# Context of one slot block in four as three float16 products of split exponentials and values

## The chip, the cores and the metric

The kernel runs on one core of a Trainium2 chip. The metric is the device time of one execution in microseconds, and for a comparison the median over several executions. One core has a matrix engine (TensorE, PE in the profile; its weight loads are listed apart as PEld), a vector engine (VectorE, DVE), an activation engine (ScalarE, ACT), a general engine (GpSimd, POOL) and a sequencer that issues transfers (SyncE, SP). Each takes its own instructions in the order that the program fixed when it was built.

## The reference

Masked self-attention on 16 batches of 1024 tokens and 512 features, with 8 heads of 64, a residual sum, and queries, keys and values all made by the same matrix.

```python
xt = jnp.transpose(x, (0, 2, 1))                  # x: (16, 512, 1024)
q = xt @ Wq.T
qh = q.reshape(B, T, NH, dk).transpose(0, 2, 1, 3)
scores = scale * jnp.einsum('bhqd,bhkd->bhqk', qh, qh)
logits = (scores * cmask + (1.0 - cmask) * NEG) * rmask
attn = jax.nn.softmax(logits, axis=-1)
ctx = jnp.einsum('bhqk,bhkd->bhqd', attn, qh)
out = ctx.transpose(0, 2, 1, 3).reshape(B, T, D) @ Wo.T
return x + jnp.transpose(out, (0, 2, 1))
```

The mask holds 0 or 1, about half of each. A token whose mask is 0 gets the mean of all values; a token whose mask is 1 attends to the tokens whose mask is 1.

## The kernel before

**Slots.** For each batch the tokens with mask 1 are gathered into at most `C` = 544 slots: four blocks of 128 (`i` = 0 to 3) and a tail of 32, 16 or 0 (`A` slots in all: 544 in the first five batches, 528 up to the fourteenth, 512 in the last two). Matrix work is done on slots alone. All other tokens get one row per batch, made from the mean.

**Batch by batch.** `run` goes through the batches in a loop. While batch b's scores and context are made, the same passage makes the queries and values of batch b + 1, normalizes and projects batch b - 1, and gathers rows for b + 2. These pieces stand in a list `m`, each with a cost, and `fill` hands them out between the steps of batch b by shares that are written out by hand. The steps `S` are (p, i): pair p of heads (0 to 3), block i (0 to 3), and two more for the tail's scores. The Tile framework then fixes the order of each engine's instructions from the program order, from priorities (`high_priority`, `behind`) and from its own estimate of when each is ready.

**Queries.** `query` (L513) makes q from float16 halves of weights and rows, three products per pair; `qsplit` (L529 to L531) splits q into a high and a low float16 half, stored as high, low, high, and four transfers spread them over the tile `xx`, whose upper 64 partitions hold the halves in the other order.

**Values.** `value` transposes q's high and low halves into PSUM (`pv`, one of the two `pm` buffers), copies it to a float32 tile `v` on ScalarE (L572) and sums squares (L556, L557). The greatest sum of squares gives the shift of the softmax, `nm` (L639), and the checks on it (`MMAX`, L644).

**Scores and exponentials.** `scores` does four float16 products (L701) into one of two PSUM buffers `pss`, and one exponential on ScalarE (L705) that reads `pss` and writes a float32 tile `p` (128 x A, 12 buffers), with the sum of each row. The tail's scores (L676) use weights of 32 columns, four matmuls side by side.

**Context.** `attend` multiplies the values of a block by its exponentials, in float32: per block four matmuls with weights of 128 x 64 (two halves of the columns `g` by two heads `k`), the two heads writing to different halves of the partitions of `pav`. The matmuls of pair p are held back and run together at step (p + 1, 1), blocks 3, 2, 1, 0 in a row; then the tail's (L730) and a copy of the result to `c` on ScalarE (L734).

**After it.** `recip_sums`, `recip_rows` and `norm` make and apply the softmax's denominators, split the context into float16 halves `ch` and `cl` (L802, L803), `project` (L817) multiplies them by the output matrix and adds the rows (L822), and indirect transfers on GpSimd's queue scatter the result (L901).

**Queues.** SP's queue takes the direct transfers in program order; `later` puts a piece of work off to the start of the next step, which so far is used for the transfers of `qsplit` and of the tail. POOL's queue takes the gathers and scatters, one per step.

Of the kernel before, what the change touches and what calls it, by code (L numbers as in the profile page):

```python
# [10 lines left out]
F32 = mybir.dt.float32  # L11
# [8 lines left out]
P = 128  # L20
D = 512
# [15 lines left out]
MMAX = 60.0  # L37
# [6 lines left out]
HPO = 300  # L44


class Fast:
# [45 lines left out]
    def setup(self, mask_t):  # L93
# [30 lines left out]
        self.oht = fixed("oht", [P, B, TB, NB], F16)  # L124
# [11 lines left out]
        self.qt = fixed("qt", [P, 2, HG, CT])  # L136
        self.number = iota("number", [P, B - 2], [[1, B - 2]], 2, 0)
# [70 lines left out]
    def permute(self):  # L208

        nc, B = self.nc, self.B - 2  # L210
        at, mh = self.at16, self.later16
        each = self.sb([P, B, TB, B], F16, "ch", 2)
        nc.vector.tensor_tensor(each, at.unsqueeze(2).broadcast_to([P, B, TB, B]),
                                mh.rearrange("p b j -> p j b").unsqueeze(1).broadcast_to([P, B, TB, B]), ALU.mult)
        with nc.allow_low_precision(reason="one of the terms is 0 or 1, the others are 0"):
            nc.vector.tensor_reduce(self.later16, each, AX.X, ALU.add)
# [15 lines left out]
    def slots(self, b0, b1):  # L232
# [13 lines left out]
        for j in range(TB):  # L246
# [22 lines left out]
                                self.ionb.unsqueeze(1).broadcast_to([P, NC, NB]), ALU.is_equal)  # L269
        for b in range(B):  # L270
            nc.vector.tensor_tensor(self.oht[:, b0 + b], oh[:, b * TB:(b + 1) * TB, :],
                                    self.tok.unsqueeze(2).broadcast_to([P, TB, NB]), ALU.mult)
# [46 lines left out]
    def index(self, b):  # L319
        nc = self.nc  # L320
        s = self.st[b]
        ol = s["ol"]
        pi = self.pm([P, NB])
        for j in range(TB):
            self.pe = nc.tensor.matmul(pi, lhsT=ol[:, j, :], rhs=self.oht[:, b, j, :], start=(j == 0), stop=(j == TB - 1)).ins
# [78 lines left out]
    def gather_now(self, b, j):  # L404
        s = self.st[b]
        if j < 4:
            s["xa"].append(self.rows(s["idx"][:, j:j + 1], self.sb([P, D], F32, "xa", 13)))
        else:
            s["xt"] = self.rows(s["idx"][:s["A"] - 512, 4:5], self.sb([P, D], F32, "xt"))
# [64 lines left out]
    def xt(self, b, k):  # L474
# [4 lines left out]
        if n:  # L479
            x = s["xa"][k] if k < 4 else s["xt"]  # L480
            if b == 0:
                pt = self.ps_s.tile([P, 2, D], F32, tag="s", name="pss")[:, 0, :DC * n].rearrange("p (c n) -> p c n", c=DC)
            else:
                pt = self.pm([P, DC, n])
            for c in range(DC):
                self.pe = nc.tensor.transpose(pt[:, c, :], x[:n, c * P:(c + 1) * P], self.ident[:n, :n]).ins
# [34 lines left out]
    def qsplit(self, b, e):  # L521
# [5 lines left out]
        full = self.sb([P, 3, C], F16, "hl", 2)  # L527
# [3 lines left out]
        nc.vector.tensor_copy(hl[:, 2, :], hl[:, 0, :])  # L531
# [6 lines left out]
        def spread():  # L538
            lo, up = slice(0, DK), slice(DK, P)
            nc.sync.dma_start(out=xx[lo, 0:2, :], in_=hl[lo, 0:2, :])  # L540
            nc.sync.dma_start(out=xx[up, 0:2, :], in_=hl[lo, 1:3, :])
            nc.sync.dma_start(out=xx[lo, 2:4, :], in_=hl[up, 0:2, :])
            self.last_xx = nc.sync.dma_start(out=xx[up, 2:4, :], in_=hl[up, 1:3, :]).ins
# [15 lines left out]
    def value(self, b, e):  # L559
# [72 lines left out]
    def bottom(self, b, g):  # L632
# [6 lines left out]
        nc.vector.tensor_scalar(nm[:, :HG], pb, -SCALE, None, ALU.mult)  # L639
# [4 lines left out]
        nc.vector.tensor_scalar(okm, nm[:, :HG], -MMAX, None, ALU.is_ge)  # L644
        nc.vector.scalar_tensor_tensor(okm, nm[:, :HG], -MMIN, okm, ALU.is_le, ALU.mult)
# [15 lines left out]
    def scores(self, b, p, i):  # L661
# [8 lines left out]
        if i is None:  # L670
# [8 lines left out]
            t = self.sb([P, C], F32, "p", 12)[:, :A]  # L679
# [24 lines left out]
        t = self.sb([P, C], F32, "p", 12)[:, :A]  # L704
# [3 lines left out]
        return t  # L708

    def attend(self, b, p, i, ps):  # L710
# [6 lines left out]
        for g in range(2):  # L717
            for k in (1, 0) if i < 4 else range(2 if A == C else 1):
                cols = slice(g * CH, (g + 1) * CH)
                if i < 4:  # L720
                    with ExitStack() as st:
                        if self.group_first:

                            st.enter_context(self.behind(self.group_first))
                            st.enter_context(self.tc.high_priority(offset=HPO))
                        mm = nc.tensor.matmul(s["pav"][k * DK:(k + 1) * DK, g, :CH], lhsT=s["v"][p][:, i, k * DK:(k + 1) * DK],  # L726
                                              rhs=ps[k][:, cols], start=(i == 3), stop=(i == 0 and A == 512))
                    self.group_first = self.group_first or mm.ins
                elif A > 512:
                    nc.tensor.matmul(s["pav"][:, g, :CH], lhsT=s["vt"][p // 2][:, k, p % 2 * 2:p % 2 * 2 + 2, :],  # L730
                                     rhs=s["pt"][:, p % 2, cols], start=False, stop=(k == 1 or A < C))
        if i == 4:
# [44 lines left out]
    def norm(self, b, p):  # L777
# [4 lines left out]
        if p == 0:  # L782

            s["ch"] = self.sb([P, NP, 512], F16, "ch", 2) if b < self.B - 1 else self.xh[:, :, :512]
            s["cl"] = self.sb([P, NP, 512], F16, "cl", 2) if b < self.B - 1 else self.xl[:, :, :512]
# [15 lines left out]
        ch, cl = s["ch"][:, p, :], s["cl"][:, p, :]  # L801
# [7 lines left out]
    def product(self, ch, cl, cols, po=None, es=range(DC)):  # L809
# [5 lines left out]
        for e in es:  # L815
            for k, (a, w) in enumerate(((ch, wh), (ch, wl), (cl, wh))):
                nc.tensor.matmul(po[:cols.stop - cols.start], lhsT=a[:, e, cols], rhs=w[:, e, :],  # L817
# [14 lines left out]
    def late(self, b, j, tag="xi", bufs=8):  # L832

        self.post(lambda: self.late_now(b, j, *(("xg", 1) if j == 4 else (tag, bufs))), urgent=j == 4)

    def late_now(self, b, j, tag, bufs):
        s = self.st[b]
        idx = s["tails"][:len(self.group[b]) * CT] if j == 4 else s["idx"][:P if j < 8 else T - self.kept[b] - 3 * P, j:j + 1]
        s.setdefault("xi", {})[j] = self.rows(idx, self.sb([P, D], F32, tag, bufs)), idx

    def project_tail(self, b, *part):
# [6 lines left out]
        po = self.product(*s["ct"], slice(0, m), *part)  # L848
# [8 lines left out]
    def project_means(self, b):  # L857
# [9 lines left out]
        po = self.product(m[:, 0], m[:, 1], slice(0, n))  # L867
# [435 lines left out]
```

## Time and profile before

| | |
|---|---|
| median of 3 runs | 1032.48 us (1032.27 to 1036.74) |
| the profiled execution's own time | 1036.56 us |
| its span, first to last instruction | 1034.9 us |
| mean granted clock of TensorE | 0.993 |
| PE busy, share of the span | 989.3 us, 96% |
| DVE busy | 724.1 us, 70% |
| ACT busy | 659.2 us, 64% |
| POOL busy | 301.5 us, 29% |

The page gives, for each engine, the time in which at least one of its instructions ran; then the span in 40 slices; then groups of instructions by line, with the busy time of the group, the mean of one, and the idle time of the engine just before them and what ended it. Matmuls overlap each other, so the mean duration of a matmul is longer than the distance from one start to the next; what a stretch of matmuls costs is read from the starts in the timeline. The answers by window give the busy time of each engine in a stretch; the answers on waits give who waited for whom.

### The profile page before, as it was taken

The numbers are of one execution on the slowest core, as the hardware profiler recorded it, in microseconds if no ns is written. First come the engines' busy times: TensorE is split into PE (matmuls) and PEld (weight loads), VectorE is DVE, ScalarE is ACT, GpSimd is POOL, SyncE is SP. The second block draws the span as 40 slices with busy tenths as digits, with TensorE's granted clock in tenths as the row PEclk, the third lists the DMA queues.
The fourth block names the chain that finished last, engine by engine and source line by source line (L and its number), as shares of the span: only waits on it lengthen the run. The fifth ranks groups of instructions, "written<-read, shape, count | busy, mean of one in ns | idle before, by whom it ended". The sixth has DMA issues, their size and how long they took to land. (4 is left out here: it accounts for less than half of the span.)

```text
span 1034.9 us, 23506 instructions
## 1 busy us (share of the span) xinstructions
PE 989.3 (96%) x8455; PEld 686.2 (66%) x8455; DVE 724.1 (70%) x2410; ACT 659.2 (64%) x1702; POOL 301.5 (29%) x307
## 2 busy tenths in 40 slices
PE   7798999999999999999999999999999999999996
PEld 6576667666676766767666676766767666676563
DVE  6897668676675667876676787767677776666653
ACT  5876667657667665667667567666667666565550
POOL 3101013222311232333232333323233232326562
PEclk9899999999999999999999999999999999999998
DMA  6846556557654485575658665576665657455652
GB/s 206 224 135 184 139 137 162 174 160 205 175 133 131 138 244 167 154 208 142 197 158 217 181 174 170 155 202 187 164 211 147 195 166 193 140 142 186 195 187 85
DMA packets 78795, 177.73 MB, mean 172 GB/s; under 512 B 14688, under 2 KB 20576, under 8 KB 78672
## 3 DMA queue, kind: packets, MB, share of 16 engines
q1 hardware_dynamic: 57584, 108.40, 39.0%
q0 software_dynamic: 21088, 67.75, 20.9%
q8 instruction: 69, 1.13, 0.5%
q14 instruction: 54, 0.44, 0.1%
HBM read 91.49 MB, written 33.91 MB: 121 GB/s over the span
## 5 line engine op out<-in xcount | busy, mean ns | idle before, releaser
L705 ACT ACTIVATE p<-pss,nm 128x528 f32<-128x528 f32 (+2 forms) x512 | 359.3, 706 | 186.5 <-PE pss L701 176.6
L701 PE MATMUL pss<-xx 128*128 128x264 f16 (+2 forms) x2048 | 302.7, 277 | 6.3 <-ACT p L705 5.2
L726 PE MATMUL pav<-p,v 128*64 128x264 f32 (+2 forms) x2048 | 243.3, 390 | 0.0
L701 PEld LDWEIGHTS <-xx 128*128 128x128 f16 x2048 | 194.9, 99 | 64.2 <-issue 26.2
L726 PEld LDWEIGHTS pav<-p,v 128*64 128x64 f32 x2048 | 141.5, 137 | 85.6 <-issue 13.5
L901 POOL DMA_INDIRECT y_out<-xa,idx x68 | 73.5, 1081 | 282.3 <-PE pss L701 100.1
L513 PE MATMUL pm<-xh,wqh 128*128 128x264 f16 (+5 forms) x512 | 142.4, 278 | 3.7 <-DVE xa L822 3.1
L513 PE MATMUL pm<-xh,wql 128*128 128x264 f16 (+5 forms) x512 | 141.9, 277 | 0.0
L513 PE MATMUL pm<-xl,wqh 128*128 128x264 f16 (+5 forms) x512 | 141.8, 277 | 0.0
L395 POOL DMA_INDIRECT xa<-x_in,idx x68 | 67.4, 992 | 208.2 <-PE pss L701 91.8
L513 PEld LDWEIGHTS <-wqh 128*128 128x128 f16 x1024 | 98.3, 99 | 23.7 <-issue 7.1
L705 ACT ACTIVATION_READ_ACCUMULATOR p<-pss,nm 128x1 f32 x512 | 104.1, 203 | 0.0
L901 POOL DMA_INDIRECT y_out<-xi,idx x60 | 73.6, 1226 | 96.7 <-PE pss L701 27.6
L817 PE MATMUL pm<-woh,ch 128*128 128x512 f16 x240 | 91.1, 380 | 0.0
L817 PE MATMUL pm<-wol,ch 128*128 128x512 f16 x240 | 91.0, 379 | 0.0
L817 PE MATMUL pm<-woh,cl 128*128 128x512 f16 x240 | 91.0, 379 | 0.0
L395 POOL DMA_INDIRECT xi<-x_in,idx x60 | 62.5, 1042 | 93.6 <-PE pss L701 31.2
L516 ACT ACTIVATE q<-pm 128x264 f32<-128x264 f32 (+5 forms) x128 | 50.1, 391 | 58.1 <-PE pm L513 57.4
L822 DVE SCALAR_TENSOR_TENSOR xa<-pm,xa 128x512 f32<-128x512 f32 x60 | 41.3, 688 | 54.3 <-PE pm L817 50.6
L817 PEld LDWEIGHTS <-ch 128*128 128x128 f16 x480 | 46.0, 98 | 44.8 <-issue 0.9
L888 DVE TENSOR_TENSOR xi<-xi,ub 128x512 f32<-128x512 f32 (+1 forms) x60 | 40.8, 687 | 42.6 <-PE pss L701 42.3
L799 DVE TENSOR_TENSOR c<-c,rb 128x528 f32<-128x528 f32 (+2 forms) x64 | 45.4, 709 | 30.0 <-PE pm L513 16.3
(223 smaller groups left out, 1506.4 us busy)
## 6 DMA issues: line engine op xcount, KB each, us to landing
xx<-hl SPq DMA_DIRECT2D x224, 136.0 KB
xm<-x_nat_in SPq DMA_DIRECT2D x56, 512.0 KB
rb<-rd SPq DMA_DIRECT2D x72, 132.0 KB
rb<-rd SPq DMA_DIRECT2D x40, 136.0 KB
pt<-c SPq DMA_DIRECT2D x36, 132.0 KB
pt<-p SPq DMA_DIRECT2D x36, 132.0 KB
ub<-ud SPq DMA_DIRECT2D x16, 256.0 KB
xx<-hl SPq DMA_DIRECT2D x32, 128.0 KB
```

What stands on the lines that cost most here:

```text
L395: dma = self.nc.gpsimd.indirect_dma_start(out=tile[:n], out_offset=None, in_=self.x, in_offset=bass.IndirectOffsetOnAxis(ap=idx, axis=0))
L513: self.beat = nc.tensor.matmul(pq, lhsT=w[:, c, e * P:(e + 1) * P], rhs=xx[:, c, cols], start=(k == 0), stop=(k == 3 * DC - 1)).ins
L516: nc.scalar.activation(s["q"][:, e, cols], pq, AF.Copy, scale=1.0 / (SX * SW))
L701: self.beat = nc.tensor.matmul(pt[:, g, :CH], lhsT=xx[:, 2 * k, i * P:(i + 1) * P], rhs=xx[:, 2 * k + a, g * CH:(g + 1) * CH], start=(a == ...
L705: self.exp = [nc.scalar.activation(t.rearrange("p (g c) -> p g c", g=2), pt[:, :, :CH], AF.Exp, bias=s["nm"][p // HG][:, p % HG:p % HG + 1 ...
L726: mm = nc.tensor.matmul(s["pav"][k * DK:(k + 1) * DK, g, :CH], lhsT=s["v"][p][:, i, k * DK:(k + 1) * DK], rhs=ps[k][:, cols], start=(i == ...
L799: self.once(nc.vector.tensor_tensor(c[:, :A], c[:, :A], s["rb"][p], ALU.mult), self.beat if p < 3 else None)
L817: nc.tensor.matmul(po[:cols.stop - cols.start], lhsT=a[:, e, cols], rhs=w[:, e, :], start=(e == 0 and k == 0), stop=(e == DC - 1 and k == 2))
L822: self.nc.vector.scalar_tensor_tensor(x, po, 1.0 / (SX * SW), x, ALU.mult, ALU.add)
L888: self.once(self.nc.vector.tensor_tensor(x[:n], x[:n], s["ub"][:n], ALU.add), self.beat)
L901: dma = self.nc.gpsimd.indirect_dma_start(out=self.out, out_offset=bass.IndirectOffsetOnAxis(ap=idx, axis=0), in_=x, in_offset=None)
```

## The change

In `attend`, block 0 of the four (`PARTS = (0,)`) is no longer one float32 product but three float16 products: high exponential by high value, high exponential by low value, low exponential by high value. The others stay in float32. The tail's products stand ahead of it in the source, and are the same.

```diff
+LIFT = 26.0 * math.log(2.0)
+UP = 2048.0
+PARTS = (0,)
-MMAX = 60.0
+MMAX = 20.0
...
 def value(self, b, e):
...
+        s.setdefault("vp", []).append(self.parts(v, pv))
...
+    def parts(self, v, pv):
+        nc = self.nc
+        n = len(PARTS)
+        t = self.sb([P, 3, n, P], F16, "vp", 6)
+        nc.scalar.activation(t[:, 0], pv[:, :n], AF.Copy, scale=UP)
+        nc.vector.scalar_tensor_tensor(t[:, 1], v[:, :n], UP, t[:, 0], ALU.mult, ALU.subtract)
+        nc.vector.tensor_scalar(t[:, 2], t[:, 0], -1.0 / UP, None, ALU.mult)
+        return t
...
 def bottom(self, b, g):
-        nc.vector.tensor_scalar(nm[:, :HG], pb, -SCALE, None, ALU.mult)
+        nc.vector.tensor_scalar(nm[:, :HG], pb, -SCALE, LIFT, ALU.mult, ALU.add)
...
 def scores(self, b, p, i):
-        t = self.sb([P, C], F32, "p", 12)[:, :A]
+        t = self.sb([P, C], F32, "p", 10)[:, :A]
...
+        if i not in PARTS:
+            return t
+        hi, lo = (self.sb([P, C], F16, k, 4)[:, :A] for k in ("ph", "pl"))
+        def split():
+            nc.scalar.activation(hi, t, AF.Copy, scale=1.0 / UP)
+            nc.vector.scalar_tensor_tensor(lo, hi, UP, t, ALU.mult, ALU.subtract)
+        self.later(split)
+        return hi, lo
...
 def attend(self, b, p, i, ps):
+            terms = [(v[:, i], ps)]
+            if i in PARTS:
+                terms = [(vp[:, j, i], [h[j // 2] for h in ps]) for j in range(3)]
+            for g in range(2):
+                cols = slice(g * CH, (g + 1) * CH)
+                for j, (w, r) in enumerate(terms):
+                    for k in (1, 0):
...
+                            mm = nc.tensor.matmul(s["pav"][k * DK:(k + 1) * DK, g, :CH], lhsT=w[:, k * DK:(k + 1) * DK],
+                                                  rhs=r[k][:, cols], start=(i == 3),
+                                                  stop=(i == 0 and A == 512 and j == len(terms) - 1))
```

The split of the exponentials is put off with `later` to the start of the step after the one that makes them; `LIFT` multiplies all exponentials by 2 to the 26th so that their halves stay in float16's range, and the denominators take the same factor.

The rest of the diff makes room for the new tiles. `qsplit` no longer stores the high half a second time (the copy at L531 is gone), and the two of its four transfers that need the halves in the other order read them with a negative step:

```diff
-        full = self.sb([P, 3, C], F16, "hl", 2)
+        full = self.sb([P, 2, C], F16, "hl", 2)
...
-        nc.vector.tensor_copy(hl[:, 2, :], hl[:, 0, :])
...
-            nc.sync.dma_start(out=xx[up, 0:2, :], in_=hl[lo, 1:3, :])
+            nc.sync.dma_start(out=xx[up, 0:2, :], in_=turned(hl[lo]))
```

`ch` and `cl` become tiles of one pair of heads each (six buffers in place of two of four pairs); `oht`, the table of token numbers, lives for one group of batches in place of all; the gathered tail rows `xt` (now in partitions 96 and up) and `xg` share one tile `xgt`; `permute`, which runs once, works in two halves.

More of the change, by code (lines that the diff above doesn't have):

```diff
@@ L211, in permute @@
         at, mh = self.at16, self.later16
[L212 to L216, printed above, removed]
+        parts = []
+        for k in range(2):
+            n = B // 2
+            each = self.sb([P, n, TB, B], F16, "tmp", 2)
+            nc.vector.tensor_tensor(each, at[:, k * n:(k + 1) * n].unsqueeze(2).broadcast_to([P, n, TB, B]),
+                                    mh.rearrange("p b j -> p j b").unsqueeze(1).broadcast_to([P, n, TB, B]), ALU.mult)
+            parts.append(each)
+        for k, each in enumerate(parts):
+            with nc.allow_low_precision(reason="one of the terms is 0 or 1, the others are 0"):
+                nc.vector.tensor_reduce(mh[:, k * n:(k + 1) * n], each, AX.X, ALU.add)
     def active(self, b0, b1):
@@ L408, in gather_now @@
         else:
-            s["xt"] = self.rows(s["idx"][:s["A"] - 512, 4:5], self.sb([P, D], F32, "xt"))
+            s["xt"] = self.rows(s["idx"][:s["A"] - 512, 4:5], self.xgt[P - CT:])
     def start(self, b):
@@ L847, in project_tail @@
         m = n if "ub" in s else n + len(group)
-        po = self.product(*s["ct"], slice(0, m), *part)
+        po = self.product(*([t[:, e] for e in range(DC)] for t in s["ct"]), slice(0, m), *part)
         if m > n:
@@ L866, in project_means @@
             nc.vector.tensor_tensor(m[:, 1, :, k], mq, m[:, 0, :, k], ALU.subtract)
-        po = self.product(m[:, 0], m[:, 1], slice(0, n))
+        po = self.product([m[:, 0, e] for e in range(DC)], [m[:, 1, e] for e in range(DC)], slice(0, n))
         us = self.sb([P, D], F32, "tmp", 2)
```

61 lines of the change are left out of this document (33 added, 28 removed).

## The prediction

> **What bounds the kernel now.** I read the page first, then what PE waits for, then the timeline of one stretch of context products, then busy times by window.
>
> ```profile
> span 1034.9 us, 23506 instructions
> PE 989.3 (96%) x8455; PEld 686.2 (66%) x8455; DVE 724.1 (70%) x2410; ACT 659.2 (64%) x1702; POOL 301.5 (29%) x307
> ...
> PE   7798999999999999999999999999999999999996
> ...
> DVE  6897668676675667876676787767677776666653
> ACT  5876667657667665667667567666667666565550
> ```
>
> PE is at nine tenths or more from the fourth slice to the last but one; DVE and ACT are far from full, but DVE reads 9 in the third slice. So PE's own work sets the end, and what can be lost is what PE waits for:
>
> ```profile
> engine line waited for: us in total, times, longest us
> PE pss L701 <- ACT p L705: 5.2, 12, 0.6
> PE pm L764 <- ACT p L705: 4.5, 6, 0.8
> PE pav L730 <- DMA pt<-p: 4.4, 4, 2.2
> ...
> PE pm L513 <- DVE xa L822: 3.1, 5, 1.0
> PE pm L764 <- DVE rcol L758: 3.1, 4, 0.9
> ```
>
> After the start, the rows of this answer that name DVE sum to 10.2 us and those that name ACT to 12.1 us. PE is hardly ever kept waiting, so a microsecond of matmuls saved is nearly a microsecond of span, and a new wait is paid in full as well.
>
> What a matmul costs is the distance between starts, from the timeline (start, length of the merged group, count):
>
> ```profile
> 505.23 0.84 PE L701 MATMUL pss<-xx 128*128 128x264 f16 x6
> 506.00 3.78 PE L726 MATMUL pav<-p,v 128*64 128x264 f32 x32
> ...
> 518.72 0.64 PE L676 MATMUL pss<-xx 128*32 128x264 f16 x16
> ```
>
> L726 shows 2048 instructions for 1024 products in the code: each float32 product is two. The 32 are 16 pairs, the two heads of a pair side by side in the two halves of the columns. Taking off the median length of one (0.386 us): 3.39 / 15 = 0.226 us a pair. The float16 row L701: (0.84 - 0.277) / 5 = 0.113 us a matmul. L676 is float16 with four matmuls side by side, weights 32 columns wide: (0.64 - 0.277) / 3 = 0.121 us for a set of four.
>
> **The change part by part.**
>
> *Products on PE.* Per pair of heads and batch (64 times) block 0 was 8 float32 instructions, 4 pairs: 4 x 0.226 = 0.905 us. Now it is 12 float16 ones, 6 pairs (2 column halves x 3 products). No row shows a float16 pair of 64 columns; the bounds are 0.113 (as L701) and 0.121 (as L676), so 0.68 to 0.73 us. It is nearest to L676, whose figure has a longer first step in it; I take 0.115, 0.69 us. Gain 0.215 us x 64 = 13.8, rounded to **-13.5** (bounds -11.2 and -14.4). The weight loads grow from 8 to 12 per pair of heads; L676 loads four sets of weights within 0.121 us, so I count them as hidden; uncovered they are priced as a rival below.
>
> [...]
>
> *Work on ACT.* 128 casts of 128x528 (`hi`): 0.60 (L734, 128x528 out of PSUM) to 0.64 us (between the two widths of L425, 0.63 at 512 and 1.05 at 1024): 82 us. 64 casts of 128x128 (`parts`): from L516 (266 wide, 0.39) and L444 (512 wide, 0.59) 0.28 us: 18 us. Together +100, from 659 to 759 us.
>
> *Work on DVE.* 128 times `lo`, like L530 (0.704 us for 128x528): 90 us. 64 times the low values, by L181 (0.417 at 256 wide, 0.682 at 512) 0.29 us: 18 us. 64 times the scaled copy, between L534 (0.17 at 48 wide) and L531 (0.29 at 528), 0.19 us: 12 us. The copy at L531 goes: -18.7 us. Net +101, from 724 to 825 us, 80%. Neither engine becomes the bound by its sum.
>
> *Where it falls.* The split runs at the start of step (p, 1), just ahead of the stretch of held back products, in which PE needs nothing new from either engine. What it finds there:
>
> ```profile
> 51.00:80.00 29.00, 28.21 (x263) 20.34 (x263) 27.78 (x100) 22.35 (x60) 1.27 (x1) 1.00 0.49 136
> 485.00:547.00 62.00, 60.73 (x530) 42.89 (x529) 44.94 (x150) 40.92 (x107) 19.61 (x18) 1.00 0.62 175
> 506.00:509.70 3.70, 3.70 (x33) 2.20 (x32) 2.35 (x7) 2.17 (x6) 1.56 (x1) 1.00 0.20 42
> 475.70:479.40 3.70, 3.70 (x34) 2.20 (x33) 3.30 (x11) 2.14 (x6) 0.85 (x1) 1.00 0.31 83
> 492.90:496.60 3.70, 3.70 (x34) 2.20 (x34) 3.62 (x18) 1.49 (x5) 0.75 (x1) 1.00 1.05 295
> ```
>
> (Columns: window, its length, busy us of PE, PEld, DVE, ACT, POOL, clock, transfers.) In three such stretches ACT has 1.5 to 2.2 us free for 1.3 us of casts: they fit. DVE has 0.1 to 1.35 us free for 1.4 us of `lo`, so some of it runs on into the next step. DVE takes its work in order, so a `lo` that waits for its cast holds what is queued behind it: L445 and L822, which give the `pm` buffers back to PE's L513 and L569, and L758, for which L764 waits. A steady batch (485 to 547) gets 6.3 us more on each engine; idle time falls from 17.1 to about 10 us on DVE and from 21.1 to 14 us on ACT. If PE's waits grew as that idle time shrinks (10.2 x 0.74 + 12.1 x 0.5), it would be +13.6 us; if the context stretch hides all, 0. I take **+4**, nearer to 0, since PE's waits show no row of the engines' work in those stretches. The 0.28 us by which `parts` holds a `pm` buffer is in this figure: PE's waits on L572 are 0.9 and 0.3 us now.
>
> *The first batches.* From 51 to 80 us DVE is busy 27.78 of 29.00. It gets two splits (2.8), two values' parts (0.96), less two copies (0.58): 3.2 us, for 1.2 us of room: **+2** (bounds 0 and 3.2). Nothing covers it there.
>
> *The rest at nothing.* The dropped copy's gain in delay is hidden: L701 and L676 wait for `xx` once, at the start. The four transfers of `qsplit` keep number and size; SP's queue is passed in the same order. The bias needs the same number of instructions. Buffers: after its split a `p` tile is free, so ten hold what twelve held. `ch`/`cl` keep six pairs for four in use. POOL's queue is not touched: its long idle time covers the shared `xgt`.
>
> **Sum:** -13.5 + 4 + 2 = -7.5 us. The profiled execution took 1036.56 us (span 1034.9 and 1.7 around it), 4.1 us over the median; its span would be 1027.4, its time 1029.1. Against the median of 1032.48: **1025.0 us**. This case's own range is 1018 (-14.4, nothing lost) to 1027.
>
> **The rivals.**
>
> *The gain is eaten.* The waits grow with the engines' load by the 13.6 us above, and the gain is at its lower figure. For it: DVE at 3.62 of 3.70. Against: 10 us of idle time per batch stay. -13.5 + 9 + 2 = -2.5: 1030 us.
>
> *DVE sets the pace behind the splits (slower).* Each `lo` waits for ACT's cast, which stands behind two exponentials (0.70 us each), and holds DVE's queue for up to 1.4 us more; the first matmul after the stretch that needs a `pm` buffer from L445 or L822 then waits. It decides from 13.5 / 64 = 0.21 us of PE wait per split on. At 0.4 us: +25.6 - 13.5 = +12, 1044.5 us. For it: the second and third stretch shown, and the slice at 9. Against: PE has 3.5 us of products to spend while the queue clears.
>
> *Loads or pairs in series (slower).* If the loads of a float16 pair (0.096 us each at L676) followed the matmuls, a pair would take 0.113 + 0.1 to 0.19, say 0.26 us: 6 x 0.26 - 0.905 = +0.66 us x 64 = +42, with the other terms 1080 us. If the two heads ran one after the other: 12 x 0.113 - 0.905 = +0.45 us x 64 = +29, 1067 us. Against both: L676 and L726.
>
> *The checks send it another way.* `MMAX` falls from 60 to 20. The shift is an eighth of the greatest sum of 64 squares of about unit size: mean 8, greatest some 16. If one batch were over it, all would be done again by the general path, at more than twice the time. Almost excluded.
>
> **Chances.** Forecast 0.55; gain eaten 0.20; DVE's pace 0.20; series 0.04; the checks 0.01. 0.5% (5.2 us) is about what a measurement of this kernel can tell from no change: faster than 1027.3 is the forecast, 0.55; within it the gain eaten, 0.20; slower the rest, 0.25. The range 1017.5 to 1043 leaves out a few hundredths below and half of the slow rival and the series above.
>
> **What would show it.** Right: a group of 24 float32 and 12 float16 instructions at `attend`, some 0.2 us shorter than 3.71 us; float16 pairs 0.113 to 0.121 us apart; ACT near 759 and DVE near 825 us; PE's busy time some 14 us less, and its waits on DVE and ACT some 5 us more, the first of them before 80 us. Wrong: pairs at 0.2 us or more, or rows "PE ... <- DVE" in which L445, L822 or L758 sum to over 14 us more.

## The result, and the profile after

The changed kernel took 1049.45 us, median of 4 runs (1046.1 to 1050.91), the kernel before on the same chip 1033.65 us (1032.27 to 1036.74): ratio 1.0127, 95% interval 1.0101 to 1.0152. By the ratio that is slower by some 13 us (the two medians lie 15.8 us apart), where 7.5 us less were forecast. A second measurement, on another chip, gave the same (e16 below: 1.0126).

The page of the changed kernel, whose profiled execution took 1046.1 us (the quickest of the four), with the slices of PE, DVE and ACT:

```profile
span 1044.4 us, 24397 instructions
...
PE 982.6 (94%) x8711; PEld 692.6 (66%) x8711; DVE 803.8 (77%) x2604; ACT 737.4 (71%) x1894; POOL 301.9 (29%) x307
...
PE   7788899999999999999999999999999998999996
...
DVE  6796967887876867988786888778778886777763
ACT  5875786767777776787777677777768776766660
```

PE's busy time is 6.7 us less and the span 9.5 us longer, so PE stands still for 16.2 us more. The second to fifth slice (26 to 131 us), which read 7, 9, 8, 9 before, read 7, 8, 8, 8. The pieces of work, by line:

```profile
L738 DVE SCALAR_TENSOR_TENSOR pl<-ph,p 128x528 f16<-128x528 f16 (+2 forms) x128 | 88.0, 701 | 3.6 <-ACT ph L737 3.2
L737 ACT ACTIVATE ph<-p 128x528 f16<-128x528 f32 (+2 forms) x128 | 77.9, 647 | 0.6
L595 ACT ACTIVATE vp<-pm 128x128 f16<-128x128 f32 x64 | 19.1, 299 | 0.0
L596 DVE SCALAR_TENSOR_TENSOR vp<-v,vp 128x128 f16<-128x128 f32 x64 | 18.3, 287 | 0.8 <-ACT vp L595 0.5
L597 DVE TENSOR_SCALAR vp<-vp 128x128 f16<-128x128 f16 x64 | 12.8, 199 | 0.0
```

In the order L738, L737, L595, L596, L597 the durations taken for them were 0.704, 0.60 to 0.64, 0.28, 0.29 and 0.19 us: each is about right. One group of held back products, in the timeline of PE:

```profile
501.53 2.89 PE L770 MATMUL pav<-p,v 128*64 128x264 f32 x24
504.25 0.40 PE L770 MATMUL pav<-ph,vp 128*64 128x264 f16 x4
504.47 0.28 PE L770 MATMUL pav<-pl,vp 128*64 128x264 f16 x2
504.58 0.40 PE L770 MATMUL pav<-ph,vp 128*64 128x264 f16 x4
504.81 0.28 PE L770 MATMUL pav<-pl,vp 128*64 128x264 f16 x2
505.02 0.29 PE L725 MATMUL pss<-xx 128*128 128x264 f16 x1
```

The 12 float32 pairs take 504.25 - 501.53 = 2.72, 0.227 us each. The 6 float16 pairs start (504.81 - 504.25) / 5 = 0.112 us apart, and the last of them 0.21 us before the next matmul. So from its start to that matmul the group lasts 505.02 - 501.53 = 3.49 us. Before, the group that starts at 506.00 lasted 3.71:

```profile
506.00 3.78 PE L726 MATMUL pav<-p,v 128*64 128x264 f32 x32
509.71 1.07 PE L701 MATMUL pss<-xx 128*128 128x264 f16 x8
```

The float16 pairs are no further apart than the matmuls of L701 (0.113 us in the prediction). The 12 weight loads of 128x64 for them (mean of all such loads at L770 110 ns) take 0.79 us in all, from 504.03 to 504.82 us, beside matmuls that run without a gap: no time of their own shows, as the prediction counted.

What PE waits for now:

```profile
PE pss L725 <- ACT p L729: 13.5, 17, 2.8
PE pav L754 <- DMA pt<-p: 6.6, 4, 2.1
PE pm L806 <- DVE nm L663: 5.4, 8, 0.7
...
PE pm L806 <- DVE rcol L800: 2.7, 4, 1.4
...
PE pm L526 <- DVE xa L865: 0.6, 2, 0.4
```

Over all rows of this answer, taken for 0 to 140 us and for the rest apart, PE waits 15.0 us before and 23.8 after in the first part (+8.8, of it ACT +6.7), and 21.0 and 27.6 in the rest (+6.6, of it DMA +4.4, DVE +2.0, ACT +0.9). The start of the sixth group of held back products, at 129.7 us before, is at 139.2 after: 9.5 us late. The last one, at 1011.8, is 9.7 us late. So in this execution 9.5 us are lost by the sixth group, which belongs to the second batch. From there on the two kernels keep step: 58 groups, each shorter by 0.215 us (the median of all 64), save 12.5 us, and as much is lost again. Of that, 6.6 us are the waits above and 1.7 us one stretch at half clock (next section); some 4 us stand in no row.

*What the first batches lose, in the timeline.* PE before, from 59 us:

```profile
59.27 0.62 PE L701 MATMUL pss<-xx 128*128 128x272 f16 x4
59.77 0.28 PE L513 MATMUL pm<-xh,wqh 128*128 128x272 f16 x1
...
61.04 0.28 PE L513 MATMUL pm<-xh,wql 128*128 128x272 f16 x1
61.15 0.27 PE L628 MATMUL pm<-ident,smcol 128*128 128x128 f32 x1
61.26 0.63 PE L701 MATMUL pss<-xx 128*128 128x272 f16 x4
```

and after:

```profile
59.24 1.10 PE L725 MATMUL pss<-xx 128*128 128x272 f16 x8
61.03 0.62 PE L725 MATMUL pss<-xx 128*128 128x272 f16 x4 [0.69 <-ACT p L729]
62.76 0.51 PE L725 MATMUL pss<-xx 128*128 128x272 f16 x3 [1.11 <-ACT p L729]
64.07 0.33 PE L806 MATMUL pm<-ident,rcol 128*128 128x128 f32 x1 [0.80 <-DVE rcol L800]
64.23 0.28 PE L526 MATMUL pm<-xh,wqh 128*128 128x272 f16 x1
```

Before, twelve matmuls of the queries (L513) stand between one set of four scores and the next, and ACT makes its exponentials meanwhile. After, fifteen matmuls of scores stand one behind the other, and the queries (L526) behind them: PE waits for ACT's exponentials, one by one, since there are two `pss` buffers. No line of the diff moves the queries: the Tile framework gave PE another order. In the first 140 us the kernel before has no run of more than 8 matmuls of scores; the changed one has three, with 38 matmuls in all. From 140 us on both have four such runs.

### The profile page after: what moved, and what is told of

Its sections match the earlier page's. It is cut to its first block, busy times and chain, and to the rows that moved or that the text cites. A ratio compares the mean times of both kernels' runs of the same rounds, so it can differ in the third digit from the quotient of the medians.

```text
span 1044.4 us, 24397 instructions
## 1 busy us (share of the span) xinstructions
PE 982.6 (94%) x8711; PEld 692.6 (66%) x8711; DVE 803.8 (77%) x2604; ACT 737.4 (71%) x1894; POOL 301.9 (29%) x307
## 5 line engine op out<-in xcount | busy, mean ns | idle before, releaser
L725 PE MATMUL pss<-xx 128*128 128x264 f16 (+2 forms) x2048 | 301.6, 277 | 14.6 <-ACT p L729 13.5
L770 PE MATMUL pav<-p,v 128*64 128x264 f32 (+2 forms) x1536 | 187.7, 394 | 0.8 <-ACT c L776 0.8
L944 POOL DMA_INDIRECT y_out<-xa,idx x68 | 76.5, 1125 | 297.3 <-PE pm L618 94.6
L770 PEld LDWEIGHTS pav<-p,v 128*64 128x64 f32 x1536 | 105.5, 138 | 66.0 <-issue 12.9
L526 PE MATMUL pm<-xh,wqh 128*128 128x264 f16 (+5 forms) x512 | 142.1, 278 | 2.5 <-DVE xa L865 0.6
L526 PE MATMUL pm<-xl,wqh 128*128 128x264 f16 (+5 forms) x512 | 141.5, 276 | 0.2 <-DVE xl L457 0.2
L526 PE MATMUL pm<-xh,wql 128*128 128x264 f16 (+5 forms) x512 | 141.7, 277 | 0.0
L526 PEld LDWEIGHTS <-wqh 128*128 128x128 f16 x1024 | 98.5, 98 | 22.2 <-issue 4.6
L944 POOL DMA_INDIRECT y_out<-xi,idx x60 | 70.5, 1175 | 90.1 <-PE pss L725 25.4
L738 DVE SCALAR_TENSOR_TENSOR pl<-ph,p 128x528 f16<-128x528 f16 (+2 forms) x128 | 88.0, 701 | 3.6 <-ACT ph L737 3.2
L865 DVE SCALAR_TENSOR_TENSOR xa<-pm,xa 128x512 f32<-128x512 f32 x60 | 41.3, 688 | 51.0 <-PE pm L860 50.3
L737 ACT ACTIVATE ph<-p 128x528 f16<-128x528 f32 (+2 forms) x128 | 77.9, 647 | 0.6
```

What stands on the lines that cost most here:

```text
L526: self.beat = nc.tensor.matmul(pq, lhsT=w[:, c, e * P:(e + 1) * P], rhs=xx[:, c, cols], start=(k == 0), stop=(k == 3 * DC - 1)).ins
L725: self.beat = nc.tensor.matmul(pt[:, g, :CH], lhsT=xx[:, 2 * k, i * P:(i + 1) * P], rhs=xx[:, 2 * k + a, g * CH:(g + 1) * CH], start=(a == ...
L737: nc.scalar.activation(hi, t, AF.Copy, scale=1.0 / UP)
L738: nc.vector.scalar_tensor_tensor(lo, hi, UP, t, ALU.mult, ALU.subtract)
L865: self.nc.vector.scalar_tensor_tensor(x, po, 1.0 / (SX * SW), x, ALU.mult, ALU.add)
L944: dma = self.nc.gpsimd.indirect_dma_start(out=self.out, out_offset=bass.IndirectOffsetOnAxis(ap=idx, axis=0), in_=x, in_offset=None)
```

## What the granted clock shows

The four runs of the changed kernel list a mean granted clock of 0.994, 0.992, 0.984 and 0.986, and spans of 1044.4, 1047.3, 1048.1 and 1049.2 us. Where the clock falls is seen by windows of e16, the same kernel (us from the start, length, busy PE, PEld, DVE, ACT, POOL, clock, transfers):

```profile
597.00:599.00 2.00, 0.00 (x0) 0.00 (x0) 1.93 (x11) 0.74 (x3) 0.91 (x1) 1.00 0.80 156
599.00:601.00 2.00, 1.87 (x12) 1.49 (x13) 0.00 (x0) 1.11 (x2) 0.00 (x0) 0.76 0.26 95
601.00:603.00 2.00, 2.00 (x11) 1.36 (x10) 0.30 (x3) 0.67 (x4) 0.00 (x0) 0.50 0.39 130
603.00:605.00 2.00, 2.00 (x20) 1.33 (x19) 1.82 (x9) 1.51 (x6) 0.94 (x1) 0.89 0.00 0
```

PE stands 2.34 us (for the tail's transfer `pt`), starts again at 599.13, and soon works some 3.4 us at half clock: 0.50 in the third row, and the last three rows together are (0.24 + 0.50 + 0.11) x 2.00 = 1.70 us short of a clock of 1.00. In the profiled execution of the change the same wait is 2.09 us long and no fall follows it. PE in e16, some way ahead of another fall, which shows as a clock of 0.53 from 64 to 66 us and 0.61 from 66 to 68:

```profile
60.17 0.62 PE L725 MATMUL pss<-xx 128*128 128x272 f16 x4 [0.70 <-ACT p L729]
61.91 0.51 PE L725 MATMUL pss<-xx 128*128 128x272 f16 x3 [1.11 <-ACT p L729]
63.21 0.33 PE L806 MATMUL pm<-ident,rcol 128*128 128x128 f32 x1 [0.80 <-DVE rcol L800]
```

The same three waits stand above in the first execution of this kernel (0.69, 1.11 and 0.80 us), and there no fall follows (clock 1.00 in every microsecond from 55 to 75 us). Another wait in that execution shows how one arises and what a fall costs. DVE, ACT and PE from 870 us:

```profile
871.88 0.71 DVE L840 TENSOR_TENSOR c<-c,rb 128x528 f32<-128x528 f32 x1 [3.46 <-DMA rb<-rd]
...
872.51 0.15 DVE L666 TENSOR_REDUCE nm<-nq 128x1 f32<-128x4 f32 x1
...
872.69 0.21 ACT L674 ACTIVATE corr<-nm 128x5 f32<-128x5 f32 x1 [3.47 <-DVE nm L666]
872.81 0.68 ACT L729 ACTIVATE p<-pss,nm 128x528 f32<-128x528 f32 x1
...
873.63 0.61 PE L725 MATMUL pss<-xx 128*128 128x264 f16 x4 [2.83 <-ACT p L729]
```

The normalization of the pair before (L840) stands in DVE's queue and waits for its transfer `rb`; the shift `nm` that the next exponentials need (L666) is queued behind it. ACT's L674 waits for that, with the exponentials behind it, and PE waits for them. Then PE's products:

```profile
874.17 4.58 PE L770 MATMUL pav<-p,v 128*64 128x264 f32 x24
```

```profile
873.60:878.60 5.00, 4.97 (x30) 2.83 (x31) 4.30 (x19) 2.81 (x7) 0.00 (x0) 0.66 0.72 170
```

24 instructions that take 2.89 us at a clock of 1.00 (from 501.53 us above) take 4.58: 1.69 us more. The clock's shortfall in this window is (1 - 0.66) x 5.00 = 1.70 us. From these two figures (1 - clock) x span is taken as an estimate of the most that a run loses to the clock; it needs no trace. The loss can be less: from 1029 to 1034.8 us of the profiled execution of the kernel before the clock reads 0.55 and no matmul runs, and that is 2.6 us of the estimate. Between executions of one kernel on one chip the time grows by about 0.9 us for each us of it, by a line fitted to all executions of the experiments. The mean of the estimate over the runs is 5.6 us for the kernel before and 12.3 us for e16 beside it. Of the 11.9 us between their mean times, up to 6.7 are the clock's by this estimate. In the profiled executions the difference is smaller: counted only where PE is busy, 4.7 us before, 5.1 and 6.8 in the two of the change, which were the quickest of their four. Ahead of the three falls shown here stand waits of PE: one of 2.34 us, one of 2.83 us, and three that sum to 2.61 us. That the waits bring the falls is the author's reading and is not shown: in the first execution one wait of 2.09 us, and the same three, have no fall behind them.

The experiments below give the median and ratio; this table splits the difference of the mean times (us) into the clock's part, which is the difference of that estimate to the runs of the kernel before on the same chip, and the rest.

| kernel | difference | clock | rest |
|---|---|---|---|
| e4, products alone | -12.0 | -1.8 | -10.3 |
| e13, and casts | -11.4 | +1.0 | -12.4 |
| e14, and low halves | -9.9 | +0.3 | -10.2 |
| e15, and values | -0.9 | +2.2 | -3.2 |
| e9, work alone | +28.0 | +6.1 | +21.9 |
| e16, the change | +11.9 | +6.7 | +5.2 |
| e3, from batch 2 | -0.8 | +1.4 | -2.2 |
| e5, no low halves in the first two batches | +8.1 | +5.8 | +2.3 |
| e10, no low halves | +8.7 | +7.0 | +1.7 |
| e17, values put off | +8.5 | +6.1 | +2.4 |
| e18, values put off, from batch 2 | -3.8 | +1.6 | -5.4 |

(e13 to e15 are e4 with one more piece of work each.)

## The experiments

"Late" below is the start of the sixth group of held back products in the profiled execution against 129.7 us in the kernel before. It holds the falls of the clock up to there (1.69 us for the one priced above), and for e9 to e12, e17 and e18 also what their chips add, on which the kernel before took some 10 us longer.

**e1.** The rest of the diff without split and products, and with twelve `p` tiles.

```diff
...
-            if i in PARTS:
+            if i in PARTS and b >= 99:
                 terms = [(vp[:, j, i], [h[j // 2] for h in ps]) for j in range(3)]
...
-        if i not in PARTS:
+        if True:
             return t
...
```

> The changed kernel without the split and without the three products: block 0 in float32 again, twelve p tiles; qsplit, permute in halves, ch/cl, oht, xgt, LIFT stay. Theory A (permute, which ran at 38 us in idle time of DVE, now runs at 60 to 65 us among work that PE waits for): 2 to 5 us over before, about 1036 to 1039, with a lag of 2 to 5 us by 140 us and none added later. Theory B (the loss is the split's load on ACT and DVE alone): within 1 us of before. Theory C (the new buffers make waits in all batches): 5 us or more over before, spread over the span.

1035.04 against 1035.28 us, ratio 0.9998 (0.998 to 1.0015). Making room costs nothing that can be measured.

**e2.** `permute` in one piece again, in a buffer that is free earlier.

```diff
...
-            each = self.sb([P, n, TB, B], F16, "tmp", 2)
...
+        each = self.sb([P, B, TB, B], F16, "xx", 5)
...
```

> The changed kernel with permute in one piece in a buffer of xx that is free from the start, so that it can run at 38 us again. Theory A: of the 9.5 us of lag that stand at 140 us, 4 to 5 go (its two products and two sums take 5.0 us of DVE), so 4 to 5 us under the changed kernel. Theory B: less than 1.5 us under it.

1050.11 against 1035.28, 1.0147 (1.0099 to 1.0196), 11.2 us late. The edit did not do what it was made for: `permute` starts at 58.8 us here and at 58.7 in e16 (38.4 in the kernel before), so nothing about its place is tested. DVE is busy 27.68 us from 51 to 80 us, but e16, the change as it is, reads 27.66 there too. e1 answers both questions. From 51 to 80 us, the changed kernel first, then e1:

```profile
51.00:80.00 29.00, 24.89 (x231) 17.87 (x230) 28.98 (x89) 22.05 (x57) 0.00 (x0) 1.00 0.38 101
51.00:80.00 29.00, 27.30 (x258) 20.01 (x257) 28.98 (x94) 21.71 (x56) 1.45 (x2) 1.00 0.48 134
```

`permute` stands there in e1 as well (from 56.8 us), DVE is as full, PE does more work, and no time is lost: neither is the cause. PE's order has its three runs of scores in e2 too, the longest of 20.

**e3.** Split and products from the third batch on. The halves, and the exponentials of block 0 in the first two batches, share one set of four buffers (also in e8 and e18).

```diff
...
-            if i in PARTS:
+            if i in PARTS and b >= 2:
...
-        if i not in PARTS:
+        if i not in PARTS or b < 2:
             return t
...
```

> The changed kernel with the split and the three products from batch 2 on; the first two batches in float32 (their block 0 stands in the room of the halves). Permute as in the changed kernel. Theory A: the permute's part of the lag stays, 4 to 5 us, the rest of the 9.5 goes: 4 to 6 us under the changed kernel. Theory B (load at the start, where DVE is full): nearly all of the 9.5 us goes, less 1.5 us of products saved there: 8 us under it. If waits in the steady batches are the loss: within 2 us of the changed kernel.

1034.61 against 1035.28, 0.9993 (0.9972 to 1.0014), 1.2 us late: the loss hangs on the split of the first two batches. DVE is as full from 51 to 80 us as in the changed kernel (28.98), and PE does 27.29 us of work there against 24.89. No run of scores is over 8.

**e4.** The kernel before, with three float16 products from constant tiles and no split; block 0's real share of the context is left out.

```diff
+        self.fv = fixed("fv", [P, 3, P], F16)
+        self.fp = fixed("fp", [P, 2, C], F16)
...
+            if i == 0:
+                terms = [(self.fv[:, j], [self.fp[:, h, :A] for h in range(2)]) for j in range(3)]
...
```

> The kernel before with block 0 as three float16 products of constant pieces; nothing is split, so the output lacks block 0's real share. All theories: what PE gains with no work on ACT and DVE, 11 to 14 us under before (float16 pairs of 0.115 to 0.13 us against 0.226 x 4). If it is under 8 us, the products themselves save less than the starts show.

1023.35 against 1035.28, 0.9887 (0.985 to 0.9925): the products save 12 us (8 to 15).

**e5, e6, e7.** In the first two batches, in turn no low halves, no casts, no parts of the values. Something that is at hand stands in for each, so that this part of the context is left out there.

```diff
+        if b < 2:
+            hi = self.sb([P, C], F16, "ph", 4)[:, :A]
+            self.later(lambda: nc.scalar.activation(hi, t, AF.Copy, scale=1.0 / UP))
+            return hi, hi
```

```diff
+            self.later(lambda: nc.vector.scalar_tensor_tensor(lo, xx[:, 0, :A], 2.0 ** -10, t, ALU.mult, ALU.min))
+            return lo, lo
...
```

```diff
+        s.setdefault("vp", []).append(self.parts(v, pv) if b > 1 else None)
...
```

> The changed kernel, but in the first two batches without the low halves of the exponentials (the high half stands in for them there, so this part of the context is not the reference's). It takes 16 x 0.70 = 11 us off DVE there; the casts stay on ACT. Theory D (DVE is full there, so its added work goes into the span): 8 to 12 us under the changed kernel. Theory E (the casts hold up ACT's exponentials, for which PE waits most): 0 to 3 us under it.

> The changed kernel, but in the first two batches without the casts on ACT: DVE's instruction for the low half runs as before, on a stand-in that is always ready, and its result stands in for both halves. It takes 16 x 0.65 = 10 us off ACT and DVE's wait for it. Theory D: 0 to 3 us under the changed kernel. Theory E: 8 to 12 us under it.

> The changed kernel, but in the first two batches the values are not split (a piece of the weights stands in for them in block 0). It takes 8 x (0.29 + 0.19) = 3.8 us off DVE and 8 x 0.28 = 2.2 us off ACT, and gives the pm buffer back 0.28 us earlier eight times. Theory D: 3 to 4 us under the changed kernel. Theory E: about 2 us. If the held pm buffer is what matters: 5 us or more.

Against 1034.79 us: e5 1043.82, 1.0074 (1.0044 to 1.0103), 3.6 us late; e6 1046.49, 1.0109 (1.0068 to 1.0149), 11.3 late; e7 1048.14, 1.0111 (1.0075 to 1.0147), 11.2 late. Only without the low halves is the start nearly right, and only there are the runs of scores gone (e6 has two, e7 three). What e5 still loses is for the most part the clock's in the table. The intervals of e6 and e7 hold the result of the change.

**e8.** e3 with less work: the low half as one operation on the same scale, no scaled copy.

```diff
-            nc.vector.scalar_tensor_tensor(lo, hi, UP, t, ALU.mult, ALU.subtract)
+            nc.vector.scalar_tensor_tensor(lo, t, 1.0 / UP, hi, ALU.mult, ALU.subtract)
...
-        nc.vector.tensor_scalar(t[:, 2], t[:, 0], -1.0 / UP, None, ALU.mult)
```

> As the run with the split from batch 2 on, and the low half is made as t/UP - hi in place of UP x hi - t, so that the scaled copy of the values (L597) is not needed: 56 x 0.19 = 11 us less on DVE in the steady batches. If the steady waits come from DVE's load: 2 to 4 us under the run from batch 2, some 1031. If not: within 1 us of it.

1043.2 against 1034.79, 1.0079 (1.0051 to 1.0107): 11.3 us of DVE's instructions less than in e3 (the scaled copies of 14 batches; its busy time falls by 6.0 us), and slower by some 9 us by the ratios. DVE waits 16.3 us for `rb` against 8.0 in e3, in the way shown at 871 us, and PE waits 15.5 us for DVE after 140 us against 9.5. Less work by the sum took more time; what put the work in this place is not shown.

**e9 to e12** ran on a chip on which the kernel before took 1044.84 us. e9 does the split and keeps the float32 products (with twelve `p` tiles, and two buffers in place of four and six for the halves and the values' parts).

```diff
-        return hi, lo
+        return t
...
-            if i in PARTS:
+            if False:
...
```

> The changed kernel with all of the split's work on ACT and DVE, but block 0 multiplied in float32 as before (the halves are made and not read; twelve p tiles, fewer buffers for the halves). If cost and gain add up: products alone gave -12, the change +15 over before, so the work alone costs 27: about 1061. If the products' order or their early release of p tiles is part of the loss: clearly under 1056.

1073.14, 1.027 (1.0229 to 1.0311). The work costs 28 us by itself, the products save 12: +16, beside the +13 that the change measured. So the sum of the two agrees with the change within the intervals: the split's work takes back more than the products save. PE's waits in e9:

```profile
PE pss L725 <- ACT p L729: 17.4, 18, 3.6
PE pav L754 <- DMA pt<-p: 7.5, 4, 2.1
```

They are the first two rows of the changed kernel, longer.

**e10.** No low halves in any batch; the high half stands in, so that their share is left out. **e11.** The split two steps later.

```diff
...
-            nc.vector.scalar_tensor_tensor(lo, hi, UP, t, ALU.mult, ALU.subtract)
```

```diff
-        self.later(split)
+        self.later(lambda: self.later(split))
```

> The changed kernel without the low half of the exponentials in all batches (the high half stands in for it, so that share of the context is left out): 88 us less on DVE, the casts stay. Theory D for all batches (DVE's added work is the loss): the 27 us of cost fall to a third, 1030 to 1034. Theory E (the casts on ACT): 1045 or more.

> The changed kernel with the split put off by two steps in place of one, so that it stands behind the stretch of held back products: the same work in another place. If the place in the queue decides (a low half ahead of what PE needs): a change of 5 us or more, down if the first place was bad. If the amount decides: within 3 us of 1049.

1054.11, 1.0082 (1.0045 to 1.0118), and 1054.13, 1.0082 (1.0056 to 1.0109). The low halves, 88 us of DVE's work, are worth some 0.4%; a later place about as much, with both intervals touching the result's. e10 gains no more than e5, which left the low halves out of two batches alone. e11 is 9.5 us late without any run of more than 8 matmuls of scores: its PE waits 3.6 and 3.7 us for `xx` at L582 and L700 in the first 140 us. (e10 and e12, on the same chip, are 3.4 and 2.6 us late.)

**e12.** The exponential written as float16 at once, two products; the share of its low half is left out.

```diff
-LIFT = 26.0 * math.log(2.0)
-UP = 2048.0
+LIFT = 15.0 * math.log(2.0)
+UP = 1.0
...
-        t = self.sb([P, C], F32, "p", 10)[:, :A]
+        t = (self.sb([P, C], F16, "ph", 4) if i in PARTS else self.sb([P, C], F32, "p", 10))[:, :A]
...
-                terms = [(vp[:, j, i], [h[j // 2] for h in ps]) for j in range(3)]
+                terms = [(vp[:, j, i], ps) for j in range(2)]
```

> Block 0's exponentials are written by ACT straight into float16 (LIFT 15 in place of 26 powers of two), with no cast and no low half, and two products with the high and the low half of the values; the share of the low half of the exponentials is left out. PE: 4 float16 pairs of 0.13 us for 4 float32 ones of 0.226, -0.385 us x 64 = -25. DVE gets 64 x 0.29 = 18 us, ACT 18, against 100 each in the change. If the work on the two engines is what ate the gain: 1010 to 1016. If any touch of the first batches costs 10 us: 1020 or more.

1034.78 against 1044.84, 0.9913 (0.9883 to 0.9943): faster than both kernels, by 10 us where some 19 to 25 were expected (its figures were for a chip with the kernel before at 1035 us). PE, DVE and ACT in its page:

```profile
PE 964.6 (94%) x8455; PEld 678.5 (66%) x8455; DVE 721.9 (70%) x2412; ACT 672.1 (65%) x1766; POOL 294.9 (29%) x307
```

PE is busy 25 us less than in the kernel before. Its waits for ACT after 140 us grew from 9.2 to 18.9 us: here, too, part of the gain is given back.

**e13, e14, e15.** e4 with one piece of the work each, its result unused: casts, low halves, values.

```diff
...
+            self.later(lambda: nc.scalar.activation(hi, t, AF.Copy, scale=2.0 ** -11))
```

```diff
...
+            self.later(lambda: nc.vector.scalar_tensor_tensor(lo, self.fp[:, 0, :A], 2.0 ** -10, t, ALU.mult, ALU.subtract))
```

```diff
...
+        nc.scalar.activation(h[:, 0], pv[:, :1], AF.Copy, scale=2048.0)
+        nc.vector.scalar_tensor_tensor(h[:, 1], v[:, :1], 2048.0, h[:, 0], ALU.mult, ALU.subtract)
+        nc.vector.tensor_scalar(h[:, 2], h[:, 0], -1.0 / 2048.0, None, ALU.mult)
```

> The products of constant pieces (e4, 0.989 of before) with the 128 casts of block 0's exponentials on ACT added, put off by one step as in the change, and not read. Theory E (ACT is what PE waits for): +10 us or more, 0.998 or over. Theory D (DVE): under +4 us, below 0.993. Theory F (the values' split and its pm buffer): the same as D here.

> e4 with the 128 low halves on DVE added, on a constant in place of the high half, not read and waiting for no cast. Theory D: +12 us or more, 1.000 or over. Theory E or F: under +6 us.

> e4 with the split of the values added (64 casts on ACT that read the pm buffer, 128 short instructions on DVE), not read. Theory F: +8 us or more, 0.996 or over. Theory D or E: under +4 us. If the three additions sum to some 28 us, the work adds up; if to much less, it is their coming together.

Against 1035.76 us: 1024.24, 0.9891 (0.9853 to 0.9929); 1025.61, 0.9911 (0.9877 to 0.9944); 1034.69, 0.9991 (0.9974 to 1.0009). Beside e4's 0.9887 the casts cost nothing that can be measured, the low halves at most a few us, the values, with the least work of the three, 0.0104 of 1035 us, 11 us, up to 4 of them the clock's in the table. The three sum to some 14 us and together they cost 25 to 28 (e16 less e4, and e9). No row of e15's waits names the values for more than 0.5 us; PE's work from 42 to 110 us in e4, and then in e15, shows a part of it:

```profile
42.00:110.00 68.00, 63.45 (x594) 46.92 (x595) 59.01 (x193) 50.86 (x132) 5.31 (x5) 0.97 0.58 155
```

```profile
42.00:110.00 68.00, 61.18 (x554) 43.87 (x554) 55.60 (x190) 47.28 (x125) 5.26 (x5) 0.94 0.55 147
```

2.3 us less of work, at a lower clock. The sixth group starts 1.2 us early in e4 and 3.8 us late in e15, the last one 13.0 and 3.9 us early.

**e16.** The changed kernel again.

> The changed kernel unaltered, as a control on this chip: 1.010 to 1.016 of before.

1046.83 against 1035.76, 1.0126 (1.0082 to 1.017).

**e17, e18.** The values' parts made from `v` in SBUF, a step later, behind the squares; e18 from the third batch on. The kernel before took 1046.09 us on this chip.

```diff
-        nc.scalar.activation(t[:, 0], pv[:, :n], AF.Copy, scale=UP)
+        def split():
+            nc.scalar.activation(t[:, 0], v[:, :n], AF.Copy, scale=UP)
...
+        self.later(split)
```

> The changed kernel with one edit: the three pieces of a value pair are made from the copy v in SBUF instead of from PSUM, one step later, behind the squares and behind what the shift's chain asks of VectorE. The amount of work is the same. If the 11 us that the split of the values cost when it stood alone come from its place (it holds one of the two pm buffers and stands ahead of the squares), about 10 us come back: ratio to the kernel before 1.001 to 1.005, and the waits of TensorE for pm fall. If they come from the work itself, the ratio stays at 1.012 to 1.013.

> The same edit, and split and product of three only from the third batch on; the first two batches keep the float32 product for the fourth block. From the third batch on alone the change stood at ratio 0.9993. If the place of the values' split and the two full first batches are separate causes, both come back: ratio 0.990 to 0.995, faster than the kernel before. If the price of the values' split lay in the first two batches only, it stays at 0.998 to 1.000.

1054.59, 1.0077 (1.0055 to 1.0099), and 1042.98, 0.996 (0.9942 to 0.9977). e17 lies between its two expectations: about 5 us come back of the 10 (its interval lies under the result's, but overlaps that of e16). So the place of the values' split, on `pm` and ahead of the squares, is about half of their price. e17 still has the three runs of scores in its first 140 us. e18 has none and is faster than the kernel before, by less than was expected; e12 does without most of the work and gains more.

## Why the prediction was wrong

*What bounds the kernel* was right: PE's own work sets the end, and new waits were paid. Behind some of them more was lost: 1.69 us at half clock behind the one of 2.83 us.

*Products on PE, -13.5.* Right. A float16 pair takes 0.112 us, at the lower of the bounds, 0.113 and 0.121, and a group is shorter by 0.215 us by the medians of all 64 (3.713 and 3.498 us), 13.8 us in all; e4 measured -12.0 (interval of the ratio: -7.8 to -15.5 us). PE's busy time, which was to fall by some 14 us, fell by 15.5 in e4 but by 6.7 in the change. The other way round, the rival of loads or pairs in series, is excluded.

*The rest at nothing.* Right for all but the ten `p` tiles: e1. Those stand in e4 as well, and cost it nothing that shows.

*The sums on ACT and DVE.* ACT stands at 737 us for 759, DVE at 804 for 825. The single durations were right (busy time counts instructions that overlap once), and neither engine is full.

*The first batches, +2 (bounds 0 and 3.2).* This step failed first. It priced the room that DVE has from 51 to 80 us. The start measured 9.5 us in the profile, and e3 shows that without the split there about 14 us of time are gone (0.9993 for 1.0127), some 5 of them the clock's in the table. DVE is no fuller there in the change than in e1 and e3 (28.98 us in all three), which lose nothing. What the step took as given was PE's order. Seven profiles (the change, e2, e6, e7, e9, e16, e17) have runs of more than 8 matmuls of scores in the first 140 us, and all seven are 9.5 to 14.2 us late. Of the twelve without such runs eleven are at most 4.8 us late (e1, e3, e4, e5, e8, e10, e12 to e15, e18), and one, e11, is 9.5 late by other waits. So the start's loss goes with the order, though the order is not the only way to lose it. That the order makes the loss is argued from the timeline and from these profiles and not shown, since no run changed the order alone; why the framework puts the queries behind the scores when split work is added is open.

*The waits on ACT and DVE, +4 (0 to 13.6).* This term was mis-sized: from the sixth group on the change loses all of the 12.5 us that its products save there, close to the upper bound, and only in part where the step looked. The rows on DVE after 140 us grew by 2.0 us and those on ACT by 0.9. Those on the transfer `pt` grew by 4.4 (by 2.2 over the whole run, since one of the four such waits of the kernel before comes earlier). And the granted clock was lower, for which the sum had no term: up to +6.7 us over the whole run (e16, by the estimate above). The prediction read PE's waits as a sum; the falls read above stand behind a wait of 2.34 us, one of 2.83 us, and three close together, and whether length and distance decide is not shown. The profiled execution of the kernel before has no fall of the clock from 60 to 1000 us (1.00 over the whole stretch).

*The 0.28 us by which `parts` holds a `pm` buffer*, put inside the +4, was too small an item: the values cost 11 us by themselves (e15, the clock's part included), and e17 puts about half of it down to their place. The other half is not settled.

*The rival of DVE's pace* gave 1044.5 us, near the time, by another mechanism: the low halves, which it made the cause, cost some 2 us where they stand alone (e14, where they wait for no cast). In the change DVE stands still for 3.2 us in all for the casts ahead of them (L738 above), where the rival had 0.4 us of PE's time for each of 64 splits, and the rows that name L457, L865 and L800 do not grow by its 14 us. *The gain is eaten* describes the batches from the third on (e3). *The checks* did not act; what the general path takes, no run here shows.

What stays open besides: why the three pieces of work together cost 25 to 28 us and by themselves 14. The runs of scores came with a part of it: e13 to e15 have none, and without the low halves (e5, e10) they are gone.

## What to carry to other kernels

Work that fits into the idle time of an engine by its sum can still cost the engine that sets the pace: here DVE was busy 804 and ACT 737 of 1044 us with it, and by itself it cost 28 us (e9). Where a scheduler builds the order from its own estimates, the order may change with the work: after such a change, read first whether the bounding engine's instructions stand in the same order, at the start above all, and only then the waits. Look at the granted clock behind waits too: here 1.69 us more were lost at half clock behind one of 2.83 us, and nothing behind one of 2.09 us. Where an engine can write the wanted type at once and the lost low half can be borne, that can beat a split that is hidden by sums: here 0.9913 (e12) against 1.0127.

## What was not expected of the hardware

After PE stood for 2.34 us (e16) or 2.83 us (the change at 870 us), and also after three waits of 0.70, 1.11 and 0.80 us between 59 and 64 us (e16), the granted clock fell to half for some 3.4 us (0.50 in the window 601 to 603 us of e16; 0.66 over 5 us behind 873.6 us, 1.70 us short of 1.00; 0.53 and 0.61 over two times 2 us from 64 us of e16, 1.72 us short). Where it was priced, at 873.6 us, that cost 1.69 us. In another execution of the same kernel it did not fall after the same three waits, nor after 2.09 us for `pt`. The four executions of the first measurement took 1046.1 us at a mean clock of 0.994, 1048.97 at 0.992, 1049.94 at 0.984 and 1050.91 at 0.986. The kernel before differed from chip to chip as well: medians of 1034.79 to 1035.76 us on three, at a mean (1 - clock) x span of 5.3 to 5.6 us, and of 1044.84 and 1046.09 on two others, at 8.6 and 10.0. By that estimate at most 3 to 5 us of these 10 are the clock's; the rest is open.
